# Attention products with W_sa by pairs of row tiles, on rows divided by their denominators when they leave PSUM

## The chip, the cores and the metric

The kernel runs on one core of one Trainium2 chip. The metric is device time in microseconds (us), the median of repeated runs. A profiled execution of the same kernel gives the trace from which all rows below are taken; its clock starts with the first instruction.

The engines are named as the profile names them: PE is TensorE (PEld its weight loads), DVE is VectorE, ACT is ScalarE, POOL is GpSimd, which also issues DMAs, and SP issues DMAs only.

## What is computed

Four graph layers on 2708 nodes with 512 features, one after the other, all in float32. Layers 0 to 2 are of the form "normalize, multiply by the adjacency matrix, multiply by a weight matrix, add". The change lies in layer 3:

```python
h = maximum(layernorm(x), 0)
attn_a = sigmoid(concat([adj @ h, h]) @ Wa.T + ba)          # one gate for each row
attn_b = sigmoid(concat([adj @ h, h]) @ Wb.T + bb)
hW = h @ W_sa
s_left, s_right = hW @ a_sa[0, :512], hW @ a_sa[0, 512:]
e = where(adj != 0, exp(-leaky_relu(s_left[:, None] + s_right[None, :], 0.01)), 0)
attn = e / (sum(e, axis=1) + 1e-5)
x_a = attn @ hW
x_b = adj @ (h @ W_gcnb) + b_gcnb
x = x + sigmoid(attn_a * x_a + attn_b * x_b)
```

The kernel uses that `attn @ (h @ W_sa)` is `(e @ h) @ W_sa` with each row divided by its sum of `e`.

## The kernel before

**Tiles.** The 2708 rows are four quarters (`NQ`) of 677. A quarter holds five full tiles of 128 rows (`KT`), and 37 rows that are left; the rows left of all quarters are gathered in two more tiles, `NF` (4 x 32 rows) and `NF + 1` (4 x 5 rows in 32). A quarter's columns are worked on in two halves (`U`) of 339 (`W`).

**The aggregation.** In each layer `aggregate` forms `adj @ h` by seven outer products instead of eight (a Strassen scheme, `multiply`), into `agg`, which holds the transposed result: features on the partitions, rows of the graph along the free axis. In layer 3 the epilogue of this aggregation is `gated`: for each row tile the products with W_gcnb and the gate vectors. It takes the full tiles two by two: `sums_of_pair` builds four sums of the two tiles' halves, `pair_product` makes seven half products with the weights and with four sums of the weights (`sums_of_w`), and combines them on VectorE (`u2`, `u3`, `c22`, `c21`, `c12`), the first one after a ScalarE copy `v`.

**The attention loop.** `steps` lists 4 quarters x 2 halves x 5 steps. A group is one quarter's half: steps b = 0 to 3 take one block each of 5 x 128 source rows, step b = 4 the tails. `e_step` loads a block of the adjacency (SP's queue, 847.5 KB) and `scores` turns it into `e` in place: ten exponentials on ScalarE (L1215), then two VectorE operations on 128x1695 (L1219, L1220). The loop makes the block of the next step before it multiplies the present one. TensorE multiplies `h` with the block into four PSUM banks `pe` (L1299, 20 matmuls of 339 columns a step), in step 4 the tails (L603, L608). VectorE adds all tiles of `e` into `se` (L1310), which gives the row sums once it is summed over the partitions. At a group's end the four banks go to `agg`, two by VectorE (L1316), two by ScalarE (L1318).

**The row tiles.** A group that ends puts its row tiles on `todo`; each following step takes one. `attention` loads the tile's x and the gated part y, sums `se` by a matmul with one column of ones (L1236), adds eps, takes the reciprocal and multiplies with the gate (L1239 to L1241), multiplies the tile of `agg` with W_sa in four matmuls of 512 columns (L203), and ends with VectorE, tanh on ScalarE, VectorE and the output DMA on POOL's queue (L1246 to L1250):

```python
sm = ps_sm.tile([P, NT], FP, tag="sm", name="pse")
nc.tensor.matmul(sm[:, 0:1], columns(t), ones[:, 0:1], start=True, stop=True)
cs = tile_cols(agg, t)
g = small.tile([P, 1], FP, tag="ge", name="ge")
nc.vector.tensor_add(g, sm[:, 0:1], eps[:, t : t + 1])
nc.vector.reciprocal(g, g)
nc.vector.tensor_mul(g, g, ga[:, t, 0:1])
```

What is left on `todo` after the loop is multiplied then, with `NF + 1` and `NF` put between; the last tile goes in two halves.

**Storage.** PSUM has eight banks: `ps_agg` five, `ps_out` two, `ps_sm` one. The blocks of the adjacency lie in `obuf`, seven places, taken from and given back to the list `free`. In the loop x and y tiles have four places in `ends`.

**Order.** A scheduler places the instructions of each engine; every engine then works through its own list in that order, and waits at an instruction whose inputs or places are not ready.

Of the kernel before, what the change touches and what calls it, by code (L numbers as in the profile page):

```python
# [12 lines left out]
P = 128  # L13
D = 512
# [23 lines left out]
def gnn_kernel(  # L38
# [60 lines left out]
    eps = const.tile([P, NT], FP, name="eps")  # L99
# [13 lines left out]
    ab_rows = dram.tile([NQ, 2, U * W], FP, name="ab_rows")  # L113
# [45 lines left out]
    def full_cols(a, t):  # L159
        k = t % KT  # L160
        return a[:, k * P : (k + 1) * P]
# [52 lines left out]
    def small_cols(tag, n):  # L214

        if n <= KT:
            return small.tile([P, KT], FP, tag=tag, name=tag)
        k = ("rs", "rq", "rv", "rstd", "sh").index(tag)
        return hd[:, :, k] if k < 4 else eps
# [815 lines left out]
    for k in range(2):  # L1035
# [10 lines left out]
    both_places = ends[:, NC * D + 2 * NC :]  # L1046
    w_sums = both_places[:, 0 : 4 * NC // 2 * GW].rearrange("p (k c o) -> p k c o", k=4, c=NC // 2)
    s_places = [
        both_places[:, o : o + 4 * NC // 2 * P].rearrange("p (k c n) -> p k c n", k=4, c=NC // 2)
        for o in (4 * NC // 2 * GW, 4 * NC // 2 * (GW + P))  # L1050
    ]
    w11, w12, w21, w22 = (wg_sb[:, f : f + 2, k] for f in (0, 2) for k in range(2))

    def sums_of_w():
        t1, t2, t3, t4 = (w_sums[:, k] for k in range(4))
        nc.vector.tensor_sub(t1, w12, w11)
        nc.vector.tensor_sub(t2, w22, t1)
        nc.vector.tensor_sub(t3, w22, w12)
        nc.vector.tensor_sub(t4, w21, t2)

    def sums_of_pair(t):
        q = t // KT, (t + 1) // KT
        (a11, a12), (a21, a22) = (
            [agg[:, f, q_ // 2, :, q_ % 2, (t_ % KT) * P : (t_ % KT + 1) * P] for f in range(2)]
            for t_, q_ in ((t, q[0]), (t + 1, q[1]))
        )
        sums_ = take(s_places)
        s1, s2, s3, s4 = (sums_[:, k] for k in range(4))
        nc.vector.tensor_sub(s3, a11, a21)
        nc.vector.tensor_add(s1, a21, a22)  # L1070
        nc.vector.tensor_sub(s2, a22, s3)
        nc.vector.tensor_sub(s4, a12, s2)
        return {1: a11, 2: a12, 3: s4, 4: a22, 5: s1, 6: s2, 7: s3}

    def pair_product(xs_):

        ws = dict(zip((1, 2, 3, 5, 6, 7, 4), (w11, w21, w22, *(w_sums[:, k] for k in range(4)))))

        def part(ps, k, start):
            for c in range(2):  # L1080
                nc.tensor.matmul(
                    ps, xs_[k][:, c], ws[k][:, c], start=start and c == 0, stop=c == 1,
                    skip_group_check=not start,
                )

        def place(tag, bufs=1):
            return upool.tile([P, W], FP, tag=tag, name=tag, bufs=bufs)[:, 0:GW]

        pa, pb, pc, pd = (
            (ps_out if k == 1 else ps_agg).tile(  # L1090
                [P, GW], FP, tag="out" if k == 1 else "agg", name=f"pp{k}"
            )
            for k in range(4)
        )
        part(pa, 1, True)
        v = place("v")
        nc.scalar.copy(v, pa)
        part(pb, 6, True)
        u2 = place("u2", 2)
        nc.vector.tensor_add(u2, v, pb)  # L1100
        part(pa, 2, False)
        part(pc, 7, True)
        u3 = place("u3")
        nc.vector.tensor_add(u3, u2, pc)
        part(pd, 5, True)
        c22 = place("s")
        nc.vector.tensor_add(c22, u3, pd)
        part(pc, 4, False)
        c21 = u3
        nc.vector.tensor_add(c21, u2, pc)  # L1110
        part(pd, 3, False)
        c12 = u2
        nc.vector.tensor_add(c12, u2, pd)
        return [[pa, c12], [c21, c22]]
# [17 lines left out]
    def gated(ts):  # L1132
        ts = list(ts)
        pairs = [t for t in ts if t < NF][::2]
        xs_ = sums_of_pair(pairs[0]) if pairs else None
        for n, t in enumerate(pairs):
            po = pair_product(xs_)
            if n + 1 < len(pairs):
                xs_ = sums_of_pair(pairs[n + 1])
            for k in range(2):  # L1140
                gates(t + k, po[k])
# [19 lines left out]
    def row_scales():  # L1161
# [8 lines left out]
        nc.vector.tensor_scalar(eps, hd[:, :, 0], srmin, None, ALU.add)  # L1170
        nc.vector.scalar_tensor_tensor(eps, eps, 0.01, eps, ALU.mult, ALU.max)
        nc.vector.tensor_sub(dinv, eps, hd[:, :, 0])
        nc.vector.scalar_tensor_tensor(dis, hd[:, :, 0], -0.01, eps, ALU.mult, ALU.add)
        nc.scalar.activation(eps, eps, AF.Exp)
        nc.vector.tensor_scalar(eps, eps, 1e-5, None, ALU.mult)
# [3 lines left out]
            po[: 2 * NT, 0:P], dd[:, 1:3].rearrange("p k t -> p (k t)"), ident,  # L1179
            start=True, stop=True,  # L1180
        )
        r = small.tile([P, P], FP, tag="diag", name="rows", bufs=2)
        nc.scalar.copy(r[: 2 * NT], po[: 2 * NT, 0:P])
        for k in range(2):
# [14 lines left out]
    def column_rows(q):  # L1199
# [4 lines left out]
        for k, r in enumerate((ra, rb)):  # L1204
            nc.vector.memset(r[:, Q : U * W], 0.0)
            nc.gpsimd.dma_start(r[:, 0:Q], ab_rows[q, k, 0:Q].partition_broadcast(P))
# [24 lines left out]
    def attention(t, columns, pieces=1):  # L1231
# [3 lines left out]
        sm = ps_sm.tile([P, NT], FP, tag="sm", name="pse")  # L1235
        nc.tensor.matmul(sm[:, 0:1], columns(t), ones[:, 0:1], start=True, stop=True)  # L1236
        cs = tile_cols(agg, t)
        g = small.tile([P, 1], FP, tag="ge", name="ge")
        nc.vector.tensor_add(g, sm[:, 0:1], eps[:, t : t + 1])  # L1239
        nc.vector.reciprocal(g, g)  # L1240
        nc.vector.tensor_mul(g, g, ga[:, t, 0:1])  # L1241
        n = D // pieces
        for k in range(pieces):
            f = slice(k * n, (k + 1) * n)
            pE = tile_product(t, cs, [wsa_sb[:, c, f] for c in range(NC)])
            nc.vector.scalar_tensor_tensor(y[:, f], pE, g, y[:, f], ALU.mult, ALU.add)  # L1246
            nc.scalar.activation(y[:, f], y[:, f], AF.Tanh, scale=0.5)
            nc.vector.scalar_tensor_tensor(xt[:, f], y[:, f], 0.5, xt[:, f], ALU.mult, ALU.add)
            for o, m, to in place(t):
                nc.gpsimd.dma_start(out[to : to + m, f], xt[o : o + m, f])  # L1250

    sums = misc[:, 0 : 2 * U * W + NQ * (R0 + R1)]
    tail_sums = sums[:, 2 * U * W :].rearrange("p (f i c q r) -> p f i c q r", f=1, i=2, c=1, q=2)
# [14 lines left out]

    steps = [(q, u, b) for q in range(NQ) for u in range(U) for b in range(NQ + 1)]
    lines, ready = {}, None  # L1270

    def gated_and_ready(ts):

        nonlocal ready
        if ts[0] < half:
            sums_of_w()
            return gated(ts)
# [3 lines left out]
        ready = e_step(*steps[0])  # L1281
# [5 lines left out]
    todo = []  # L1287
    for n, (q, u, b) in enumerate(steps):
        cu = slice(u * W, (u + 1) * W)
        se = sums[:, (q % 2) * U * W : (q % 2 + 1) * U * W]  # L1290
        if b == 0:
            pe = [ps_agg.tile([P, W], FP, tag="agg", name=f"pe{c}") for c in range(NC)]
            if u == 1 and q + 1 < NQ:
                lines[q + 1] = column_rows(q + 1)
        (now, blks), ready = ready, e_step(*steps[n + 1]) if n + 1 < len(steps) else None
        if b < NQ:
            for c in range(NC):
                for t, a in now:
                    nc.tensor.matmul(  # L1299
                        pe[c], h[:, t, c * P : (c + 1) * P], a, start=(t == 0), stop=False  # L1300
                    )
        else:
            tail_products(pe, now, False)
            now = [(NF, now[:, 0, :]), (NF + 1, now[:G, 1, :])]
        for t, a in now:
            if t == 0:
                nc.vector.tensor_copy(se[:, cu], a)
            else:
                r = G if t == NF + 1 else P
                nc.vector.tensor_add(se[:r, cu], se[:r, cu], a)  # L1310
        free.extend(blks)
        if b == NQ:
            for c in range(NC):
                d = agg[:, c // 2, q // 2, c % 2, q % 2, cu]
                if c % 2 == 0:
                    nc.vector.tensor_copy(d, pe[c])  # L1316
                else:
                    nc.scalar.copy(d, pe[c])  # L1318
            if u == 0:
                todo += [(t, se) for t in range(q * KT, q * KT + W // P)]  # L1320
            else:
                nc.vector.tensor_copy(tail_sums[:, 0, q // 2, 0, q % 2], se[:, KT * P : Q])
                todo += [(t, se) for t in range(q * KT + W // P, (q + 1) * KT)]
        elif todo:
            t, se_t = todo.pop(0)
            attention(t, lambda t, se_t=se_t: full_cols(se_t, t))
# [3 lines left out]
    todo = [(t, lambda t, se_t=se_t: full_cols(se_t, t)) for t, se_t in todo]  # L1330
    for k, t in ((1, NF + 1), (3, NF)):
        todo.insert(k, (t, lambda t: tile_cols(tail_sums, t, True)[0]))
    for n, (t, columns) in enumerate(todo):
        attention(t, columns, 1 if n + 1 < len(todo) else 2)
# [61 lines left out]
```

## Time and profile before

| | |
|---|---|
| median of three runs | 2083.27 us (2081.92 to 2083.51) |
| the profiled execution's own time | 2079.3 us |
| its span, first to last instruction | 2077.5 us |
| mean granted TensorE clock | 0.998 |
| attention loop, after the gates | about 1614 to 2053 us |
| last matmul of the loop to the end of the span | 24.3 us |

How to read the rows: in a group of instructions stand the line of the kernel, the engine, the operation, the names out<-in, shapes and count, then busy time in us and mean ns of one, then the engine's idle time just before them and what ended it. In a timeline stand start and length in us, and idle time with its releaser in brackets. A float32 matmul leaves two records on PE, so a count of 8 is four matmuls. The ends of matmuls are modelled, so the distance of starts is the better measure of their cost.

### The profile page before, as it was taken

The numbers are of one execution on the slowest core, as the hardware profiler recorded it, in microseconds if no ns is written. First come the engines' busy times: TensorE is split into PE (matmuls) and PEld (weight loads), VectorE is DVE, ScalarE is ACT, GpSimd is POOL, SyncE is SP. The second block draws the span as 40 slices with busy tenths as digits, with TensorE's granted clock in tenths as the row PEclk, the third lists the DMA queues.
The fourth block names the chain that finished last, engine by engine and source line by source line (L and its number), as shares of the span: only waits on it lengthen the run. The fifth ranks groups of instructions, "written<-read, shape, count | busy, mean of one in ns | idle before, by whom it ended". The sixth has DMA issues, their size and how long they took to land.

```text
span 2077.5 us, 19986 instructions
## 1 busy us (share of the span) xinstructions
PE 2035.2 (98%) x7246; PEld 1264.6 (61%) x7246; DVE 1429.1 (69%) x2521; ACT 407.8 (20%) x828; POOL 193.9 (9%) x350
## 2 busy tenths in 40 slices
PE   5999999999999999999999999999999999999998
PEld 2566655656666554666664556666677666666665
DVE  4678877666767778766686889968759755565512
ACT  1430001130000011100002120000117533444411
POOL 0111111120000011100002130001001001000011
PEclk9999999999999999999999999999999999999999
DMA  9998594554445353655444565544552323233220
GB/s 369 304 379 265 184 344 178 190 191 168 168 161 182 137 178 135 238 169 169 160 163 156 197 225 188 175 154 161 188 188 105 119 98 120 93 105 102 96 69 27
DMA packets 80771, 363.65 MB, mean 175 GB/s; under 512 B 11140, under 2 KB 16172, under 8 KB 80544
## 3 DMA queue, kind: packets, MB, share of 16 engines
q1 hardware_dynamic: 50672, 245.43, 33.7%
q0 software_dynamic: 30000, 116.95, 17.3%
q8 instruction: 57, 0.93, 0.2%
q14 instruction: 42, 0.34, 0.1%
HBM read 297.38 MB, written 62.17 MB: 173 GB/s over the span
## 4 chain that ended last, share of the span: by engine, by line
PE 81%; issue 8%; DVE 5%; DMA 5%; POOL 1%; ACT 0%; SPq 0%; POOLq 0%; DVEq 0%; ACTq 0%
PE pe L1299 17%; PE pc L541 13%; PE pa L541 13%; PE pd L541 13%; PE po L203 12%; PE pb L541 6%; DMA obuf<-in_yb_dram 3%; PE pt L603 3%; PE pe L603 1%; PE pt L608 1%; DMA osumt<-ends 1%; DVE ends L1004 1%; DMA ends<-xs 1%; PE dg_ps L324 1%; POOL xbs L1130 0%
## 5 line engine op out<-in xcount | busy, mean ns | idle before, releaser
L1299 PE MATMUL pe<-obuf,h 128*128 128x339 f32 x1280 | 371.4, 448 | 0.0
L1299 PEld LDWEIGHTS pe<-obuf,h 128*128 128x128 f32 x1280 | 241.4, 189 | 130.5 <-issue 12.3
L541 PE MATMUL pa<-obuf,h 128*128 128x339 f32 x1040 | 317.0, 449 | 2.5 <-ACT h L255 1.4
L203 PE MATMUL po<-ends,agg 128*128 128x512 f32 (+1 forms) x648 | 281.1, 590 | 0.3 <-DVE agg L1316 0.3
L541 PEld LDWEIGHTS pa<-obuf,h 128*128 128x128 f32 x1040 | 195.3, 189 | 109.7 <-issue 9.2
L203 PEld LDWEIGHTS po<-ends,agg 128*128 128x128 f32 x648 | 121.3, 190 | 142.7 <-issue 136.5
L1215 ACT ACTIVATE e<-r,nsr 128x339 f32<-128x339 f32 x352 | 171.5, 565 | 54.4 <-DMA r<-ab_rows 15.9
L541 PE MATMUL pb<-t,s 128*128 128x339 f32 x560 | 171.2, 452 | 1.7 <-DVE s L473 0.9
L541 PE MATMUL pc<-t,h 128*128 128x339 f32 x560 | 169.4, 448 | 1.1 <-DVE u L588 1.0
L541 PE MATMUL pd<-t,s 128*128 128x339 f32 x560 | 169.0, 447 | 0.0
L541 PE MATMUL pd<-obuf,s 128*128 128x339 f32 x550 | 166.3, 448 | 0.3 <-DVE agg L562 0.3
L575 ACT COPY v<-pa 128x339 f32<-128x339 f32 x56 | 24.6, 440 | 720.9 <-PE pa L541 694.7
L541 PEld LDWEIGHTS pb<-t,s 128*128 128x128 f32 x560 | 106.2, 191 | 57.3 <-DVE t L513 2.1
L541 PEld LDWEIGHTS pc<-t,h 128*128 128x128 f32 x560 | 105.8, 189 | 56.1 <-DVE u L588 2.2
L541 PEld LDWEIGHTS pd<-t,s 128*128 128x128 f32 x560 | 105.8, 189 | 54.1
L541 PEld LDWEIGHTS pd<-obuf,s 128*128 128x128 f32 x550 | 104.0, 189 | 53.9 <-DVE agg L562 1.1
L541 PE MATMUL pc<-obuf,s 128*128 128x339 f32 x450 | 135.9, 448 | 0.0
L541 PEld LDWEIGHTS pc<-obuf,s 128*128 128x128 f32 x450 | 85.1, 189 | 43.8 <-issue 0.5
L935 POOL DMA_DIRECT2D xs<-ends x66 | 36.0, 546 | 780.8 <-DVE ends L934 705.1
L513 DVE TENSOR_TENSOR t<-obuf,t 128x1695 f32<-128x1695 f32 x55 | 105.3, 1915 | 0.0
L514 DVE TENSOR_TENSOR t<-obuf,t 128x1695 f32<-128x1695 f32 x52 | 99.5, 1914 | 0.1
L1316 DVE COPY agg<-pe 128x339 f32<-128x339 f32 x16 | 7.5, 507 | 133.1 <-PE pe L608 133.1
(290 smaller groups left out, 2280.3 us busy)
## 6 DMA issues: line engine op xcount, KB each, us to landing
obuf<-in_yb_dram SPq DMA_DIRECT2D x132, 847.5 KB, 4.5
obuf<-osumt SPq DMA_DIRECT2D x100, 847.5 KB, 4.4
osumt<-obuf POOLq DMA_DIRECT2D x22, 847.5 KB, 11.3
xs<-ends POOLq DMA_DIRECT2D x66, 256.0 KB, 2.3
ends<-xs POOLq DMA_DIRECT2D x61, 256.0 KB, 3.6
obuf<-in_yt_dram SPq DMA_DIRECT2D x28, 339.0 KB, 3.5
obuf<-in_yb_dram POOLq DMA_DIRECT2D x11, 847.5 KB, 10.9
ends<-in_yb_dram SPq DMA_DIRECT2D x9, 847.5 KB, 9.1
```

The source lines that it names most:

```text
L203: nc.tensor.matmul(po, cs[c], ws[c], start=(c == 0), stop=(c == NC - 1))
L324: nc.tensor.matmul(ps[g], first, y, start=n < 4, stop=n >= len(ops) - 4)
L513: nc.vector.tensor_add(t2, o22, t1)
L514: at_y.append(nc.vector.tensor_add(t4, o21, t2).ins)
L541: last = nc.tensor.matmul(ps, x[:, k, :], y[:, k, :], start=start and k == 0, stop=k == KT - 1, skip_group_check=not start,)
L575: at_v.append(nc.scalar.copy(v, pa).ins)
L603: nc.tensor.matmul(ps[c], h[:, NF, c * P : (c + 1) * P], tl[:, 0, :], start=start, stop=False)
L608: nc.tensor.matmul(ps[c], h[g, NF + 1, c * P : (c + 1) * P], tl[g, 1, :], start=False, stop=True)
L935: nc.gpsimd.dma_start(xs[t], xt)
L1004: nc.vector.tensor_tensor_reduce(y, h[:, t, :], vs[:, k, :], 1.0, 0.0, ALU.mult, ALU.add, hd[:, t, k : k + 1])
L1215: nc.scalar.activation(e[:, k], row, AF.Exp, bias=nsr[:, t, s : s + 1], scale=1.0)
L1299: nc.tensor.matmul(pe[c], h[:, t, c * P : (c + 1) * P], a, start=(t == 0), stop=False)
```

## The change

The full tiles' products with W_sa go by pairs with seven half products, as the gates do. For this the rows have to be divided before the product: a group's sum over the partitions is one matmul of a 128x128 matrix of ones with `se`, its reciprocal `rrow` lies on all partitions, and all four evictions from PSUM become multiplications with it on VectorE. The eps of each row goes with the `ab_rows` into DRAM and is added as a row (`erow`) to `se`. A pair's parts stand between the four main products of one step (`next(pair)`); they use `ps_sm` (`pb`, `pd`, and the sum) and `ps_out` (`pa`, `pc`). The sums of `e` are made as soon as the block is ready, and the tails together with the next group's first block. Two of the seven places of `obuf` hold the sums of W_sa from step 2 on. Six full tiles, `NF + 1` and `NF` are multiplied after the loop, instead of three and these two. The numbers of lines move: the exponentials to L1225, `scores` to L1229 and L1230, the pair's parts to L1077, the results to L1250 to L1256, the main products to L1359, the sum, its reciprocal and the evictions to L1375, L1376 and L1379.

The core of the diff:

```diff
+    def in_four(a):
+        return a.rearrange("p (k c o) -> p k c o", k=4, c=NC // 2)
+    def weights_of_pairs(w, sums):
+        w11, w12, w21, w22 = (w[:, f : f + 2, k] for f in (0, 2) for k in range(2))
+        t1, t2, t3, t4 = sums
         nc.vector.tensor_sub(t1, w12, w11)
         nc.vector.tensor_sub(t2, w22, t1)
         nc.vector.tensor_sub(t3, w22, w12)
         nc.vector.tensor_sub(t4, w21, t2)
+        return {1: w11, 2: w21, 3: w22, 4: t4, 5: t1, 6: t2, 7: t3}
...
-    def pair_product(xs_):
+    def pair_product(xs_, ws, bank):
...
+        pa = bank("pa", n)
         part(pa, 1, True)
         v = place("v")
         nc.scalar.copy(v, pa)
+        pb = bank("pb", n)
         part(pb, 6, True)
         u2 = place("u2", 2)
         nc.vector.tensor_add(u2, v, pb)
+        yield
         part(pa, 2, False)
+        pc = bank("pc", n)
         part(pc, 7, True)
         u3 = place("u3")
         nc.vector.tensor_add(u3, u2, pc)
+        yield
+        pd = bank("pd", n)
         part(pd, 5, True)
         c22 = place("s")
         nc.vector.tensor_add(c22, u3, pd)
+        yield
         part(pc, 4, False)
         c21 = u3
         nc.vector.tensor_add(c21, u2, pc)
         part(pd, 3, False)
         c12 = u2
         nc.vector.tensor_add(c12, u2, pd)
-        return [[pa, c12], [c21, c22]]
+        yield [[pa, c12], [c21, c22]]
...
         nc.tensor.matmul(
-            po[: 2 * NT, 0:P], dd[:, 1:3].rearrange("p k t -> p (k t)"), ident,
-            start=True, stop=True,
+            po[: 3 * NT, 0:P], dd.rearrange("p k t -> p (k t)"), ident, start=True, stop=True
         )
...
-        for k in range(2):
+        for k in range(3):
             for q in range(NQ):
                 t = k * NT + q * KT
                 nc.gpsimd.dma_start(
...
+    def loads(t):
         xt = load_x(t, xs)
         y = load_x(t, xbs)
         nc.scalar.activation(xt, xt, AF.Copy, bias=0.5)
-        sm = ps_sm.tile([P, NT], FP, tag="sm", name="pse")
-        nc.tensor.matmul(sm[:, 0:1], columns(t), ones[:, 0:1], start=True, stop=True)
+        return xt, y
+    def result(t, xt, y, parts, f):
+        for g, c in parts:
+            nc.vector.scalar_tensor_tensor(
+                y[:, g], c, ga[:, t, 0:1], y[:, g], ALU.mult, ALU.add
+            )
+        nc.scalar.activation(y[:, f], y[:, f], AF.Tanh, scale=0.5)
+        nc.vector.scalar_tensor_tensor(xt[:, f], y[:, f], 0.5, xt[:, f], ALU.mult, ALU.add)
+        for o, m, to in place(t):
+            nc.gpsimd.dma_start(out[to : to + m, f], xt[o : o + m, f])
...
+    def pair_bank(name, n):
+        pool, tag = (ps_sm, "sm") if name in ("pb", "pd") else (ps_out, "out")
+        return pool.tile([P, n], FP, tag=tag, name=name)
+    def attention_of_pair(ts):
+        xys = [loads(t) for t in ts]
+        xs_ = sums_of_pair(ts, e_places)
+        yield
+        halves = [slice(k * (D // 2), (k + 1) * (D // 2)) for k in range(2)]
+        for po in pair_product(xs_, ws_e, pair_bank):
+            if po is not None:
+                for t, (xt, y), ps in zip(ts, xys, po):
+                    result(t, xt, y, list(zip(halves, ps)), slice(0, D))
+            yield
...
+        last = n >= len(steps) - NQ - 1
+        pair = None
         if b == 0:
             pe = [ps_agg.tile([P, W], FP, tag="agg", name=f"pe{c}") for c in range(NC)]
+            m = min(W, Q - u * W)
+            nc.gpsimd.dma_start(
+                erow[:, 0:m], ab_rows[q, 0, u * W : u * W + m].rearrange("(o w) -> o w", o=1)
+            )
...
+        elif len(todo) >= 2 and (b == 3 if last else b in (1, 2)):
+            pair = attention_of_pair([todo.pop(0), todo.pop(0)])
+            next(pair)
+            if last:
+                pair, last_pair = None, pair
+        now, blks = ready.pop(0)
         if b < NQ:
+            make_ready(n + 1)
+            if b == NQ - 1:
+                make_ready(n + 2)
             for c in range(NC):
                 for t, a in now:
                     nc.tensor.matmul(
                         pe[c], h[:, t, c * P : (c + 1) * P], a, start=(t == 0), stop=False
                     )
+                if pair is not None:
+                    next(pair)
...
+            else:
+                tl = ready[0][0]
+                sums_of_e(se, [(NF, tl[:, 0, :]), (NF + 1, tl[:G, 1, :])])
+                nc.vector.tensor_add(se[0:1], se[0:1], erow)
         else:
+            ps = ps_sm.tile([P, W], FP, tag="sm", name="pse")
+            nc.tensor.matmul(ps, ones, se, start=True, stop=True)
+            nc.vector.reciprocal(rrow, ps)
             tail_products(pe, now, False)
+            for c in range(NC):
+                nc.vector.tensor_mul(
+                    agg[:, c // 2, q // 2, c % 2, q % 2, cu], pe[c], rrow
+                )
...
-                if c % 2 == 0:
-                    nc.vector.tensor_copy(d, pe[c])
-                else:
-                    nc.scalar.copy(d, pe[c])
...
+        if n == 2:
+            flat = [free.pop(0).rearrange("p k w -> p (k w)") for _ in range(2)]
+            places = [flat[0][:, k * D : (k + 1) * D] for k in range(3)] + [flat[1][:, 0:D]]
+            ws_e = weights_of_pairs(
+                wsa_sb.rearrange("p c (k o) -> p c k o", k=2),
+                [a.rearrange("p (c o) -> p c o", c=NC // 2) for a in places],
+            )
...
-    for n, (t, columns) in enumerate(todo):
-        attention(t, columns, 1 if n + 1 < len(todo) else 2)
+    for _ in last_pair:
+        pass
+    for k in range(2):
+        for _ in attention_of_pair([todo.pop(0), todo.pop(0)]):
+            pass
+        if k == 0:
+            attention(NF + 1)
+    attention(NF, 2)
```

## The prediction

> **What bounds the kernel now.** I read the busy table first, then the slices, then the attention stage by window, by group and in order of time, and the last 25 us in order of time.
>
> ```profile
> PE 2035.2 (98%) x7246; PEld 1264.6 (61%) x7246; DVE 1429.1 (69%) x2521; ACT 407.8 (20%) x828; POOL 193.9 (9%) x350
> ...
> 1617.00:2053.00 436.00, 436.00 (x1517) 273.83 (x1515) 220.08 (x351) 165.23 (x338) 32.91 (x61) 1.00 0.28 92
> ```
>
> The second line is the attention loop: window, TensorE, weight loads, VectorE, ScalarE, POOL, granted clock, DMA share. TensorE is busy in all 436 us at full clock; VectorE in half of them. So in the loop a matmul saved is time saved, as long as nothing new makes TensorE wait. Its course (start, length; two records for each fp32 matmul):
>
> ```profile
> 1993.68 2.44 PE L603 MATMUL pe<-tl,h 128*128 128x339 f32 x8
> 1996.05 0.85 PE L608 MATMUL pe<-tl,h 32*128 32x339 f32 x8
> 1996.83 11.70 PE L1299 MATMUL pe<-obuf,h 128*128 128x339 f32 x40
> 2008.37 0.28 PE L1236 MATMUL pse<-ones,ends 128*128 128x1 f32 x2
> 2008.51 3.68 PE L203 MATMUL po<-ends,agg 128*128 128x512 f32 x8
> 2012.03 11.59 PE L1299 MATMUL pe<-obuf,h 128*128 128x339 f32 x40
> ...
> L1246 DVE SCALAR_TENSOR_TENSOR ends<-po,ge,ends 128x512 f32<-128x512 f32 x17 | 12.7, 746 | 15.0 <-PE po L203 15.0
> ```
>
> A tile's attention takes TensorE from 2008.37 to 2012.03: 0.14 for the sum, 3.52 for four products of 512 columns, 3.66 in all. The last line counts such tiles inside the loop: 17; the other five come after it. A step's 20 matmuls of 339 columns take 11.43 (0.571 each), the two rows of the tails 3.15. The price of a half product stands in the gates, which already work by pairs:
>
> ```profile
> 1500.68 1.03 PE L1081 MATMUL pp<-ends,agg 128*128 128x257 f32 x4
> 1501.55 1.03 PE L1081 MATMUL pp<-ends 128*128 128x257 f32 x4
> 1502.42 1.03 PE L1081 MATMUL pp<-ends,agg 128*128 128x257 f32 x4
> ```
>
> Starts lie 0.87 apart: two matmuls of 257 columns. Now the end:
>
> ```profile
> 2052.34 0.85 PE L608 MATMUL pe<-tl,h 32*128 32x339 f32 x8
> 2067.42 3.70 PE L203 MATMUL po<-ends,agg 128*128 128x256 f32 x16
> ...
> 2063.05 2.02 POOL L1250 DMA_DIRECT2D out_dram<-obuf  x4 [2.12 <-DVE ge L1241]
> 2072.86 0.55 POOL L1250 DMA_DIRECT2D out_dram<-obuf  x1 [0.36 <-DVE obuf L1248]
> ```
>
> The loop's last matmul ends at 2053.2 (call it T0), TensorE's last at 2071.1 (T0+17.9), the span at 2077.5 (T0+24.3), 4.6 after the last output's issue.
>
> **The change, part by part.** The sum is made against the profiled execution (span 2077.5, its own time 2079.3); the median of the runs is 2083.3, 4 higher, and I take the difference over to it.
>
> *Products in the loop.* Before: 17 x 3.66 = 62.2. After: seven pairs (the eighth is begun, but multiplied after the loop), each seven half products of 0.87, 6.07; together 42.5. Added: eight times one matmul of `ones` with `se`, 339 columns, 0.57 as the main matmuls: 4.6. So 47.1: **-15.1**.
>
> *After the loop.* Three pairs, `NF+1` and `NF` stand here now, for five tiles before. TensorE's own work: 18.2 + 2.1 (its rows before, 1.0 and 1.05) + 3.5 = 23.8. In the built order I walk VectorE with the durations of the trace (0.42 for 128x256, pitch 0.35; 0.51 for 128x339, pitch 0.43; 0.48 for a result on 256 columns). The first pair's `u2` is queued behind four evictions, four copies of tail columns and the four sums of the next pair: it ends at T0+4.0, while TensorE has used up `pa`, `pb`, `pa`, `pc` at 3.5 and needs the single `sm` bank: 0.6 lost. `c22` behind `u3` and two more sums costs 0.2, `pa` and `pc` of the third pair 0.2: TensorE ends at about T0+24.8. Last is now `NF` in two halves, each with four output DMAs of 0.51 on POOL; the first four start at T0+25.1 behind its VectorE and ScalarE steps, so the eighth starts at 28.7, and with the same 4.6 the end is T0+33.3: **+9.0**.
>
> *Evictions.* Before, two on VectorE (0.51) and two on ScalarE (0.44); after, four on VectorE, times `rrow`. The next group's first bank is the fifth of `ps_agg`, so its second product, 2.86 after T0, is the first to need an evicted bank, done at T0+0.5. Cost 0, cover 2.3.
>
> *The reciprocal.* Before it has one column (159 ns); now `rrow` has 339. The trace has two that are larger:
>
> ```profile
> 125.72 0.23 DVE L225 RECIPROCAL dd<-hd 128x12 f32<-128x12 f32 x1 [0.29 <-ACT hd L224]
> 154.16 0.28 DVE L225 RECIPROCAL dd<-hd 128x22 f32<-128x22 f32 x1
> ```
>
> Ten more columns cost 55 ns, 5.5 ns each: 0.28 + 317 x 5.5 = 2.0. The Trainium skill speaks against it more loudly: VectorE: DVE Perf Modes, section "Walkthrough: the 8-slice pipeline in each mode", has a reciprocal as an iterative divide with a repeat count of 8; at the page's 0.96 GHz that is 8.3 ns a column, 3.0 in all by this estimate. The low bound is a plain pass, 0.5. It starts when the sum ends, 3.15 before T0, beside the tails. By the row it is ready at T0-1.1, by the page at T0-0.1: both cost nothing. From 3.05 on it delays the end, from 5.4 on also each next group. I take 2.0.
>
> *VectorE's load.* For each group it gains two evictions (1.0), the reciprocal (2.0), the row with eps (0.5), and for a pair 4 sums and 5 combinations of 0.42, 4 results of 0.48 and 2 of 0.69, 7.1, for 3.8 of two tiles' results and small operations. About 6.8 a group, 54 in all, and 2.8 once for W_sa's sums: some 277 of 421, 66%. Not the bound, so 0; what matters is order in its queue (first rival).
>
> *Waits inside a pair's step.* Counted from the step's start on TensorE: `pa`, `pb` end at 4.6, `pa`, `pc` at 9.2, `pd` begins at 12.1, `pc` at 15.8, `pd` again at 16.7. VectorE has first `L1229` for a block whose load can start only when TensorE has freed it at 0 (five blocks now, two hold W_sa's sums). In this stage such loads landed (the loads of `obuf`, 1560 to 2050) in
>
> ```profile
> DMA to landing us min/median/max: 4.1/4.4/4.6
> ```
>
> so `L1229` runs 4.6 to 6.5, `u2` ends at 7.0, `u3` at 10.3, `c22` at 13.5. Needed at 12.1, 15.8 and 16.7. `v` stands on ScalarE behind five exps whose buffer is free before the step: ready at 4.2, needed at 7.5. Cost 0; the smallest cover is 3.2. Each us beyond a cover would come in all seven pairs. Where VectorE itself waits for a pair's part, the scores of later blocks stand behind it; with five blocks these are three steps (34 us) ahead of TensorE, so nothing starves, and a pair's step is 17.5 long.
>
> *The rest, at nothing.* Six more `ab_rows` DMAs (0.54 each on POOL, which is 9% busy and ahead of need by a whole outer product); the `erow` DMA, in POOL's order before the outputs of the pair, issued a group ahead (late, it would hold `se`, the sum on TensorE and all of VectorE's queue, us for us, in eight groups); a pair's four loads, which take all four places and so wait for the last pair's output: free about 6 after a pair, needed a step later. ScalarE's 22 additions and tanhs are as many as before. TensorE's order up to the first attention product is the old one.
>
> **Sum.** -15.1 + 9.0 = -6.1: 2083.3 - 6.1 = **2077.2**.
>
> **Rivals.**
> 1. *Slower: the load ahead of `u2`.* VectorE serves in order, and `u2` frees the only `sm` bank. If the load before `L1229` takes longer than 4.5 + 5.1 = 9.6, `pd` waits, in seven pairs. For it: two blocks fewer, and loads of this size took 9.1 (SP into `ends`) and 10.9 (POOL) earlier in the kernel. Against: 4.4 in this stage at 28% DMA share. At 10.5 the gain is gone (0.9 x 7); at 12 it is 2.4 x 7 = 17 - 6: 2094. Chance 0.10.
> 2. *No change: the combinations hold TensorE a little everywhere.* Before, nothing on TensorE waited for the tile's result; now three links of each pair do, and after the loop nothing covers them. One more us for each pair behind the loop and 0.2 in the loop: 3 + 1.4, 2081.6. For it, one such wait for `v` in the gates:
>
> ```profile
> 1562.81 1.13 PE L1081 MATMUL pp<-ends,agg 128*128 128x257 f32 x4 [1.69 <-ACT v L1097]
> ```
>
> Against: the four pairs that follow it run on without a gap. Chance 0.22.
> 3. *More: the tail costs only TensorE's work.* Without its 1.0 of waits, and with outputs issued 1.5 sooner: 2074.7. Chance 0.08.
>
> The forecast itself (2074.5 to 2079.1) has 0.60.
>
> **Numbers.** 0.2% (4.2 us) is about what a measurement of this kernel can tell from no change. Faster by more: 0.60 + 0.08 = 0.68; within: 0.22; slower: 0.10. The range 2073.8 to 2082.8 takes in the third rival's better half and most of the second.
>
> **What would show it.** In the loop TensorE still at 100%, pairs as rows of four records 0.87 apart between main products, `pse` with 0.57; loop shorter by 15. `L1376` near 2.0, over before the tails' last row. After T0 about 33 instead of 24, one gap of about 0.6 before `pd`. Wrong would be: gaps before `pd` or `pc` in the loop with VectorE's `u2`, `u3` or ScalarE's `v` as releaser (rivals 1, 2), or a reciprocal over 3.

## The result, and the profile after

The changed kernel takes 2076.81 us (median of 16 runs, 2074.32 to 2082.03) against 2082.84 us of the kernel before (16 runs): a ratio of 0.9972, 95% interval 0.9964 to 0.9980, that is 5.8 us less (4.2 to 7.5). The prediction was 6.1 less. The profiled executions have 2074.84 and 2079.3, spans 2073.0 and 2077.5. The spans differ by 4.5 only, since this execution reached the attention loop 0.9 later; 54 us after its start it was already 1.9 behind the other, in instructions that the change doesn't touch. So I compare stages: the loop, from its first main product after the gates to the end of its last tail product (T0), and what lies behind T0.

| | before | after | difference | predicted |
|---|---|---|---|---|
| loop, us | 439.1 | 423.9 | -15.2 | -15.1 |
| T0 to TensorE's last product | 17.9 | 25.0 | +7.0 | +6.9 |
| T0 to the end of the span | 24.3 | 34.1 | +9.8 | +9.0 |
| the two stages | 463.4 | 458.0 | -5.4 | -6.1 |

First the busy table and two windows of the profile after (window, TensorE, weight loads, VectorE, ScalarE, POOL, granted clock, DMA share, GB/s). The second is the loop, the third what follows it:

```profile
PE 2027.9 (98%) x7338; PEld 1285.3 (62%) x7338; DVE 1495.6 (72%) x2593; ACT 406.1 (20%) x822; POOL 202.2 (10%) x367
...
1615.00:2039.00 424.00, 424.00 (x1570) 286.47 (x1569) 277.26 (x406) 164.20 (x333) 36.03 (x67) 1.00 0.30 99
2039.00:2064.00 25.00, 24.64 (x110) 18.68 (x110) 22.15 (x57) 6.11 (x12) 5.31 (x10) 1.00 0.14 53
```

TensorE is busy in all 424 us of the loop at full clock, as it was in the longer one; VectorE went from 223 of 439 to 277 of 424. One pair in the loop, TensorE in order of time (start, length, then line, operation and shapes):

```profile
1948.07 1.02 PE L1077 MATMUL pa<-ends,agg 128*128 128x256 f32 x4
1948.93 1.03 PE L1077 MATMUL pb<-obuf,ends 128*128 128x256 f32 x4
1949.80 3.02 PE L1359 MATMUL pe<-obuf,h 128*128 128x339 f32 x10
1952.66 1.02 PE L1077 MATMUL pa<-ends,agg 128*128 128x256 f32 x4
1953.52 1.03 PE L1077 MATMUL pc<-obuf,ends 128*128 128x256 f32 x4
1954.39 3.02 PE L1359 MATMUL pe<-obuf,h 128*128 128x339 f32 x10
1957.24 1.03 PE L1077 MATMUL pd<-obuf,ends 128*128 128x256 f32 x4
1958.11 3.02 PE L1359 MATMUL pe<-obuf,h 128*128 128x339 f32 x10
1960.97 1.03 PE L1077 MATMUL pc<-obuf,agg 128*128 128x256 f32 x4
1961.83 1.03 PE L1077 MATMUL pd<-ends 128*128 128x256 f32 x4
...
1985.54 0.73 PE L1375 MATMUL pse<-ends,ones 128*128 128x339 f32 x2
```

Seven rows of four records, each 0.87 up to the next row, between main products that leave no gap; `pse` takes 0.57 up to the tails behind it (1986.11). Beside it VectorE, in the same step:

```profile
1950.01 1.93 DVE L1229 SCALAR_TENSOR_TENSOR obuf<-obuf,e 128x1695 f32<-128x1695 f32 x1 [0.96 <-ACT e L1225]
1951.85 0.41 DVE L1092 TENSOR_TENSOR u<-v,pb 128x256 f32<-128x256 f32 x1
...
1954.83 0.41 DVE L1098 TENSOR_TENSOR u<-u,pc 128x256 f32<-128x256 f32 x1
...
1958.31 0.42 DVE L1103 TENSOR_TENSOR s<-u,pd 128x256 f32<-128x256 f32 x1 [1.00 <-PE pd L1077]
```

Subtract the ends from the starts on TensorE and the covers can be read off: `u2` (L1092) ends at 1952.26 and `pd` needs it at 1957.24, 5.0 to spare; `u3` (L1098) at 1955.24 for 1960.97, 5.7; `c22` (L1103) at 1958.73 for 1961.83, 3.1. The end of the last group on VectorE, then the end of the kernel on TensorE and on POOL:

```profile
2035.89 2.28 DVE L1376 RECIPROCAL ends<-pse 128x339 f32<-128x339 f32 x1 [39.80 <-PE pse L1375]
2038.93 0.93 DVE L1379 TENSOR_TENSOR agg<-pe,ends 128x339 f32<-128x339 f32 x2 [0.76 <-PE pe L608]
```

```profile
2042.79 1.13 PE L1077 MATMUL pd<-obuf 128*128 128x256 f32 x4 [0.22 <-DVE u L1092]
2060.25 3.62 PE L203 MATMUL po<-ends 128*128 128x256 f32 x16
```

```profile
2064.38 3.95 POOL L1256 DMA_DIRECT2D out_dram<-obuf  x8 [0.74 <-DVE obuf L1254]
```

The reciprocal is over 0.76 before the tails are. `pd` waits 0.22 behind the loop. The eight outputs of `NF` go out one after the other, 0.49 each, the last from 2067.84 on (T0+28.9), and the span ends 5.1 after that.

### The profile page after: what moved, and what is told of

It is laid out like the page before. It is cut to its first block, busy times and chain, and to the rows that moved or that the text cites. A ratio compares the mean times of both kernels' runs of the same rounds, so it can differ in the third digit from the quotient of the medians.

```text
span 2073.0 us, 20307 instructions
## 1 busy us (share of the span) xinstructions
PE 2027.9 (98%) x7338; PEld 1285.3 (62%) x7338; DVE 1495.6 (72%) x2593; ACT 406.1 (20%) x822; POOL 202.2 (10%) x367
## 4 chain that ended last, share of the span: by engine, by line
PE 88%; DVE 5%; DMA 4%; issue 1%; ACT 0%; POOL 0%; SPq 0%; POOLq 0%; DVEq 0%; ACTq 0%
PE pe L1359 17%; PE pa L541 14%; PE pc L541 14%; PE pd L541 14%; PE po L203 9%; PE pb L541 7%; PE pt L603 3%; DMA obuf<-in_yb_dram 2%; PE pd L1077 2%; PE pa L1077 2%; PE pc L1077 1%; DMA ends<-in_yt_dram 1%; PE pt L608 1%; PE pe L603 1%; PE pb L1077 1%
## 5 line engine op out<-in xcount | busy, mean ns | idle before, releaser
L1359 PE MATMUL pe<-obuf,h 128*128 128x339 f32 x1280 | 373.2, 448 | 0.0
L1359 PEld LDWEIGHTS pe<-obuf,h 128*128 128x128 f32 x1280 | 241.4, 189 | 121.8 <-issue 4.1
L541 PEld LDWEIGHTS pa<-obuf,h 128*128 128x128 f32 x1040 | 196.2, 190 | 110.2 <-issue 10.3
L203 PE MATMUL po<-ends,agg 128*128 128x512 f32 x480 | 207.5, 593 | 0.0
L1225 ACT ACTIVATE e<-r,nsr 128x339 f32<-128x339 f32 x352 | 172.4, 566 | 178.2 <-DVE obuf L1229 87.1
L575 ACT COPY v<-pa 128x339 f32<-128x339 f32 x56 | 24.7, 441 | 719.0 <-PE pa L541 693.0
L203 PEld LDWEIGHTS po<-ends,agg 128*128 128x128 f32 x480 | 90.9, 190 | 114.3 <-issue 109.5
L1229 DVE SCALAR_TENSOR_TENSOR obuf<-obuf,e 128x1695 f32<-128x1695 f32 x32 | 61.5, 1923 | 58.8 <-DMA obuf<-in_yb_dram 39.8
```

The source lines that it names most:

```text
L203: nc.tensor.matmul(po, cs[c], ws[c], start=(c == 0), stop=(c == NC - 1))
L541: last = nc.tensor.matmul(ps, x[:, k, :], y[:, k, :], start=start and k == 0, stop=k == KT - 1, skip_group_check=not start,)
L575: at_v.append(nc.scalar.copy(v, pa).ins)
L1225: nc.scalar.activation(e[:, k], row, AF.Exp, bias=nsr[:, t, s : s + 1], scale=1.0)
L1229: nc.vector.scalar_tensor_tensor(b, b, 0.0, e1[:, :n], ALU.not_equal, ALU.min)
L1359: nc.tensor.matmul(pe[c], h[:, t, c * P : (c + 1) * P], a, start=(t == 0), stop=False)
```

## Experiments

The forecast's theory: the loop gives back TensorE's time, because every new wait has other products in front of it, and behind the loop TensorE's work, small waits and the issue of eight outputs take 9 back. The rivals: VectorE (by its load or its order) holds `pd` and `pc`; the reciprocal is too long; or the gain comes from elsewhere. Comparisons over several runs are given as ratios to the kernel before on the same chip, whose median was 2082.8 to 2084.2; single profiled executions are read by their stages.

### The division alone

```
-        elif len(todo) >= 2 and (b == 3 if last else b in (1, 2)):
-            pair = attention_of_pair([todo.pop(0), todo.pop(0)])
+        if b < NQ and todo:
+            attention(todo.pop(0))
...
+    for k, t in ((1, NF + 1), (3, NF)):
+        todo.insert(k, t)
+    for n, t in enumerate(todo):
+        attention(t, 1 if n + 1 < len(todo) else 2)
```

> The division at the eviction alone: matmul of ones with se, reciprocal of 339 columns, four evictions on VectorE; every tile is multiplied by itself with the whole of W_sa, as before, seven blocks stay in use. My theory: the eight matmuls of 339 columns (8 x 0.57 = 4.6) less the 17 sums of one column that fall away in the loop (17 x 0.14 = 2.4), so +2.2 in the loop, and -0.7 behind it (five such sums): +1.5 against the kernel before, about 2084.3, ratio 1.0007. The pairs alone are then worth about -7.5. If instead the gain came from the division (no scale of the scores' sums by tile, results that read PSUM without it), this kernel is as fast as the changed one, 2077, ratio 0.997, and the pairs are worth nothing. If the four evictions on VectorE hold the next group, +4 or more, with gaps ahead of the main products of a new group.

Measured: ratio 0.9996 (0.9988 to 1.0004; 13 runs, 2083.9), the loop 439.9, from T0 to the end 24.4. The gain is the pairs'. The loop grew by 0.8 where 2.2 was expected. TensorE in order of time, this kernel:

```profile
1954.39 11.60 PE L1354 MATMUL pe<-obuf,h 128*128 128x339 f32 x40
1965.82 3.60 PE L203 MATMUL po<-ends,agg 128*128 128x512 f32 x8
1969.25 11.59 PE L1354 MATMUL pe<-obuf,h 128*128 128x339 f32 x40
```

A tile takes 3.43 here; before, with its sum of one column, 3.66. So that sum cost 0.23 and not the 0.14 between the two starts: the product behind it was 0.09 longer as well. 17 x 0.23 = 3.9 against 8 x 0.57 = 4.6 is the +0.7. It also tells what a pair is worth by itself: 6.07 against 2 x 3.43 = 6.86, so 0.79, and 7.9 of TensorE's work for ten pairs. Most of the loop's -15.2 is work carried out of it: three tiles, 10.3.

### Plain products behind the loop, twice

```
-        elif len(todo) >= 2 and (b == 3 if last else b in (1, 2)):
+        elif len(todo) >= 2 and not last and b in (1, 2):
...
-    for _ in last_pair:
...
+    for k, t in ((4, NF + 1), (7, NF)):
+        todo.insert(k, t)
+    for n, t in enumerate(todo):
+        attention(t, 1 if n + 1 < len(todo) else 2)
```

> Pairs inside the loop only; the six tiles that the three pairs behind the loop multiply are multiplied one by one there. The loop is then the changed kernel's (423.9 by its trace). My theory: TensorE has 26.6 of work behind the loop instead of the changed kernel's 25.0, so the end comes 1.6 later than in the changed kernel: 2078.4. That is: the three pairs keep most of their gain (9 half matmuls' worth, 3.7, of which some 2 goes to waits and to the order of the end). The rival (the pair's chain of combinations, which nothing covers behind the loop, eats its gain there): no difference, 2076.8 within 0.5, or faster.

Measured: ratio 0.9999 (0.9991 to 1.0007), 5.6 above the changed kernel's ratio where 1.6 was expected. The loop is 423.9, all is lost behind it (T0 to the end 41.1, so 7.0 more than in the changed kernel in this execution). POOL and ScalarE, then TensorE in order of time, then two windows of this kernel:

```profile
2058.18 0.54 POOL L916 DMA_DIRECT2D obuf<-xs  x1 [2.35 <-DMA out_dram<-obuf]
2061.17 0.63 ACT L1244 ACTIVATE obuf<-obuf 128x512 f32<-128x512 f32 x1 [2.73 <-DMA obuf<-xs]
```

```profile
2059.07 1.06 PE L206 MATMUL po<-ends 128*32 128x512 f32 x8
2062.84 2.08 PE L210 MATMUL po<-ends,all_again 128*128 128x512 f32 x2 [2.70 <-ACT ends L208]
2064.71 9.19 PE L203 MATMUL po<-ends,agg 128*128 128x512 f32 x16
```

```profile
2060.00:2065.00 5.00, 2.30 (x7) 1.13 (x4) 1.37 (x6) 1.62 (x3) 0.56 (x2) 0.72 0.33 128
2065.00:2070.00 5.00, 5.00 (x8) 1.94 (x8) 1.40 (x2) 0.63 (x1) 2.01 (x4) 0.60 0.05 14
```

A load stands on POOL until an output has left its place; ScalarE, in order, stands in that tile's addition (L1244) until the load has landed, ahead of `NF+1`'s copy (L208); TensorE waits 2.70 for the copy and is granted 0.72 and 0.60 of its clock in these two windows, so that the next two tiles take 9.0 instead of 6.9 (2064.71 to the next row's start at 2073.73). The edit had brought a wait of its own. The second version takes that away:

```
+        elif last and b == 3:
+            early = {t: loads(t) for t in todo[:2]}
...
-        xt, y = loads(t)
+        xt, y = early[t] if t in early else loads(t)
```

> The kernel with pairs inside the loop only once more, with the loads of the first two tiles behind the loop issued in the loop's last step, as the changed kernel does for its last pair; in the first version two loads waited for places that outputs still held, ScalarE stood in those loads ahead of NF+1's copy, TensorE waited 2.7 and was then granted 0.60 of its clock for a while. With that gone, my theory: a plain tile takes 3.43 by the trace of the kernel with the division alone, so six of them 20.6, against 18.2 for three pairs plus some 1.2 of waits: TensorE's end at T0+26.2 against T0+25.0, the whole +1.2 against the changed kernel, ratio to the kernel before 0.9978. The rival (the chain of combinations eats the pairs' gain behind the loop): 0.9972 or less. If the first version's loss was not the load's doing, it stays at 0.9999.

Measured: ratio 0.9982 (0.9974 to 0.9989; 21 runs), 0.0010 or 2.1 us above the changed kernel's; by the traces 2.2 (T0 to the end 36.3 against 34.1, loops equal). Expected was 1.2. TensorE's end came at T0+27.4; the other 1.2 is mostly one wait, here in TensorE's waits from the gates to the end:

```profile
PE po L210 <- ACT ends L208: 1.0, 1, 1.0
```

Without it the kernel is at 26.4, near the 26.2 that I had walked. So by the traces three pairs behind the loop are worth 1.4 even with nothing to cover their combinations, out of 2.4 that TensorE's work gives (3 x 0.79): the rival that these eat all of the gain there falls. The two intervals (0.9964 to 0.9980 and 0.9974 to 0.9989) still touch; the size rests on the traces.

### The outputs on two queues, and other banks

```
-        for o, m, to in place(t):
-            nc.gpsimd.dma_start(out[to : to + m, f], xt[o : o + m, f])
+        for k, (o, m, to) in enumerate(place(t)):
+            queue = nc.sync if t == NF and k % 2 else nc.gpsimd
+            queue.dma_start(out[to : to + m, f], xt[o : o + m, f])
```

> The eight output DMAs of NF alternate between POOL and SP; all else is the changed kernel. My theory: the end is set by the issue of these eight on one queue (0.49 each, the eighth at T0+28.95 by the changed kernel's trace, then 5.1 until the end). On two queues the last issue comes at T0+27.1: -1.9, 2074.9. If the end is set by the landing of the last transfer and not by the queue of issues (the DMA engines serve the eight one after the other at the same pace), no change, 2076.8.

Measured: ratio 0.9957 (0.9944 to 0.9970; 6 runs, 2074.0); loop 423.9, TensorE's end at T0+25.0 as in the changed kernel, the end of the span at T0+32.1 instead of 34.1: -2.0 by the trace, and 1.5 thousandths (3.1 us) by the ratios, whose intervals overlap. POOL now issues two of the second half's four in 0.98, the last of them from 2065.22 (T0+27.3):

```profile
2064.73 0.98 POOL L1257 DMA_DIRECT2D out_dram<-obuf  x2 [0.28 <-DVE obuf L1254]
```

So the queue of issues set the end, and not the transfers one after the other; 4.8 still follow the last issue. The second kernel has this and:

```
+        if behind_loop and name in ("pb", "pd"):
+            return ps_agg.tile([P, n], FP, tag="agg", name=name)
```

> As the kernel with the outputs on two queues, and in addition the products pb and pd of the pairs behind the loop take the banks of ps_agg, which are free there, instead of the single bank of ps_sm, so that pd need not wait for u2 nor the next pair's pb for c12. My theory: the waits behind the loop amount to about 1.2 (25.0 until TensorE's end against 23.8 of work), and most of it goes: TensorE ends near T0+24.0, 0.5 to 1.0 less than with two queues alone, about 2074.2. If the waits come from the combinations themselves (pc after u3, pb after v) and not from the single bank, no difference to two queues alone: 2074.9.

Measured: ratio 0.9953 (0.9941 to 0.9965; 5 runs), TensorE's end at T0+24.7, the span's at T0+31.8: 0.3 less than with two queues alone, less than expected. The wait of `pd` for `u2` is gone, but others remain. TensorE in order of time, this kernel:

```profile
2044.75 1.03 PE L1077 MATMUL pd<-obuf 128*128 128x256 f32 x4
2045.86 1.14 PE L1077 MATMUL pc<-obuf,agg 128*128 128x256 f32 x4
2046.99 1.13 PE L1077 MATMUL pd<-ends,obuf 128*128 128x256 f32 x4
```

Starts lie 1.11 and 1.13 apart, not 0.87: the second `pc` and the second `pd` accumulate in banks that `u3` and `c22` have just read (on VectorE these end at 2045.81 and 2046.93, 0.05 and 0.06 earlier). That is the chain itself. The same kernel on more runs:

> The kernel with the outputs on two queues and the banks of ps_agg behind the loop a second time, on more runs, because its first time rests on five. From the traces it ends 31.75 behind the loop's last matmul and the changed kernel 34.09, with loops of equal length: 2.3 faster than the changed kernel, ratio to the kernel before 0.9972 - 0.0011 = 0.9961. If the first ratio (0.9953) was luck, it is between 0.996 and 0.997; if the outputs on two queues bring nothing beyond the trace's run, 0.9972.

Measured: 0.9963 (0.9951 to 0.9975; 8 runs, 2074.1), T0 to the end 31.8 again. So the first ratio was in part luck, and the ratios alone don't tell this kernel from the one with the outputs on two queues (0.9957). By the traces it ends soonest behind the loop of all versions here, 2.3 sooner than the changed kernel; by this ratio it is 7.7 below the kernel before.

### The reciprocal twice

```
             nc.vector.reciprocal(rrow, ps)
+            nc.vector.reciprocal(rrow, ps)
```

> The reciprocal of 339 columns is issued twice in a row. My theory: 2.28 more on VectorE in each of the eight groups; the first one leaves 0.76 to spare ahead of the end of the tails. In the loop the cover is 3 and more, so its length stays 423.9 within 0.3; behind the loop, where the pairs begin at once, the evictions come 2.28 - 0.76 = 1.5 later and with them u2 and all that follows: the end at T0+35.6 instead of T0+34.1. If the reciprocal were already at its limit in each group, as the estimate of 3.0 would nearly have it, the loop would grow by up to 8 x 1.5 = 12.

Measured: loop 423.91, the changed kernel's to the hundredth; T0 to the end 34.9, +0.8 (1.5 was expected). VectorE and TensorE in order of time, this kernel:

```profile
2040.12 2.28 DVE L1377 RECIPROCAL ends<-pse 128x339 f32<-128x339 f32 x1
2042.51 1.76 DVE L1380 TENSOR_TENSOR agg<-pe,ends 128x339 f32<-128x339 f32 x4
```

```profile
2042.46 1.13 PE L1077 MATMUL pb<-obuf 128*128 128x256 f32 x4 [0.57 <-DVE ends L1377]
```

The second one ends 1.6 after T0 (2040.83), and the evictions begin 1.7 after T0, where in the changed kernel they begin with it. The pair that stands there multiplies tiles of an earlier group, so its products don't need the late columns; `pb` does need the bank that `pse` had, and TensorE begins it 1.70 behind `pa` instead of 0.97: that is nearly all of the 0.8. In the loop the delay is covered, as the prediction had it (to 5.4); what I had not seen is that the first price behind the loop is for `pse`'s bank, not for the evictions.

### VectorE's load

```
-        nc.vector.scalar_tensor_tensor(b, b, 0.0, e1[:, :n], ALU.not_equal, ALU.min)
+        for _ in range(2):
+            nc.vector.scalar_tensor_tensor(b, b, 0.0, e1[:, :n], ALU.not_equal, ALU.min)
```

The second kernel has `range(3)`.

> The first operation of the scores on a block (1.92 each, with no change to its result) is done twice: some 61 us more on VectorE, all of it in the loop, where it is then busy about 340 of 424. My theory: no wait of TensorE, the loop 423.9 within 0.5, since u2, u3 and c22 have 5.0, 5.7 and 3.1 to spare by the changed kernel's trace. If VectorE's load were already what bounds the loop (a second rate beside TensorE's), the loop grows, by up to 7 x 1.9 = 13.

> The same operation three times: some 122 us more, VectorE busy about 400 of 424. My theory: u2 comes 3.85 later and has 5.0 to spare, c22 is at its limit, and a block's chain (scores 7.7, exps 4.8) is about as long as the 13.2 that TensorE takes for a block: 0 to +10 in the loop. If VectorE binds in the loop well before it is full: +20 and more.

Measured: loop 424.9 (+1.0) with VectorE busy 337 of 425, and 430.4 (+6.5) with 387 of 430. TensorE's waits of the second kernel, from the gates to the end:

```profile
PE pe L1360 <- DVE agg L1380: 3.2, 3, 1.4
PE pd L1077 <- DVE s L1103: 2.7, 3, 2.0
```

At 79% load VectorE costs next to nothing (0.8 of the 1.0 is `pd`'s second wait, for `c22`, the smallest cover); at 90% it costs 6. Where it shows first is what the covers say: `c22`, with 3.1 to spare, and the evictions, but not `u2`, which had 3.85 of its 5.0 taken. The load is no second rate in the loop at the change's 65%.

### One wait in doses

`u2` computed 5 and 13 times in each pair of the loop, TensorE's products held in the changed kernel's order; then 13 times with the order left to the scheduler.

```
-        nc.vector.tensor_add(u2, v, pb)
+        for _ in range(times):
+            nc.vector.tensor_add(u2, v, pb)
...
+                with tc.issue_after(of_pair[-1]):
                     for t, a in now:
                         nc.tensor.matmul(
```

> In the seven pairs of the loop u2 is computed five times in a row (no change to its result), with the products of TensorE held in the changed kernel's order, so that nothing steps in where pd waits. In VectorE's order the four repeats take other work between them, so that u2 comes about 4.4 later than in the changed kernel, where it had 5.0 to spare. My theory: no wait, the loop 423.9 within 1. If pd were already at its limit (the wait for the single bank as a rate of its own), the loop grows by 7 x 4.4 = 31.

> The same with u2 computed thirteen times: 12 x 0.33 = 4.0 of repeats and up to 4.8 of other work between them, so u2 ends about 3.7 after the time at which pd is due. My theory, which is the first rival's price beyond its cover: pd waits 3.7 in each of seven pairs, the loop +26, named as a wait of pd for u. If the pairs' waits can be made up later in the step (TensorE has other products to go on with), the loop grows by less than 10.

> u2 thirteen times as before, but with the scheduler free to order TensorE's products: in the order that it makes, pd, pc and pd come eight main products later (4.6 us), behind the first products of the next step. My theory: u2 is there 0.9 before pd, no wait, the loop 423.9 within 1.5, though u2 is as late as in the kernel with the order held. If the lateness of u2 itself were what costs, the loop grows as with the order held, by 26.

Measured: 5 times, no wait in the loop, 424.5 (the 0.6 is one main product more between the loop's bounds); `u2` ends 0.2 to 1.9 ahead of `pd`. 13 times with the order held, 462.3: +38 where 26 was expected. 13 times in a free order, 425.7: +1.8, of which 1.5 is one wait of `pd`. The held kernel, TensorE's waits in the loop and one of the seven in order of time:

```profile
PE pd L1079 <- DVE u L1096: 22.7, 7, 3.9
```

```profile
1671.62 3.02 PE L1365 MATMUL pe<-obuf,h 128*128 128x339 f32 x10
1678.36 2.07 PE L1079 MATMUL pd<-obuf,ends 128*128 128x256 f32 x4 [3.72 <-DVE u L1096]
1680.23 3.60 PE L1365 MATMUL pe<-obuf,h 128*128 128x339 f32 x10
```

The waits are 22.7, 3.2 each, for the 3.7 that I had walked; the order was not held in full, since in four of the seven pairs the next pair's `pa` (0.87) stepped in ahead of the waiting `pd`. Most of the other 15.6 stands in the rows: `pd` takes 2.07 instead of 1.03, and the ten records behind it 3.60 instead of 3.02. The same stretch by windows, with the granted clock third from the end of the row:

```profile
1676.00:1678.00 2.00, 0.00 (x0) 0.00 (x0) 1.83 (x6) 0.00 (x0) 0.00 (x0) 0.99 0.00 0
1678.00:1680.00 2.00, 1.64 (x4) 1.37 (x5) 0.73 (x2) 0.00 (x0) 0.00 (x0) 0.50 0.00 0
1680.00:1682.00 2.00, 2.00 (x7) 1.26 (x6) 0.91 (x2) 0.00 (x0) 0.00 (x0) 0.65 0.00 0
1682.00:1684.00 2.00, 2.00 (x9) 1.40 (x8) 0.00 (x0) 0.00 (x0) 0.00 (x0) 1.00 0.00 0
```

After the wait TensorE runs on at half its clock for about 3 us. From `pd`'s start to that of the next `pc` the seven pairs take 5.3 to 6.3 instead of 3.73 (1957.24 to 1960.97 above), 13.0 in all: 1.9 for each wait, on top of it. The rest of 2.6 is 0.16 more from start to start at each wait than the idle time shows (1.1), one main product more between the bounds as in the kernel with five (0.6), and the eighth pair's first `pa`, which came into the loop (0.9). So the first rival is real as a mechanism, and its place (`pd`'s single bank) and its start (the cover) were right; it is dearer than I had priced it. And it doesn't come about by VectorE being slow alone: where the scheduler may move `pd`, it puts eight main products in front, and the same lateness of `u2` costs 1.8.

## Why the prediction was right, by its steps

- *Products in the loop*: -15.1 predicted, -15.2 measured. Each unit was right: 0.87 for a half product, 6.07 for a pair, 0.57 for `pse`. The division alone was put down at +2.2 in its experiment and is +0.8, since a tile's sum of one column costs 0.23; the prediction had used the whole 3.66 and was not touched by that.
- *Waits in a pair's step*: none in the loop. `u2` had 5.0 to spare (predicted 5.1), `c22` 3.1 (3.2). I had `L1229` wait for its load alone. In four of the seven pairs, the one shown above among them, what it waited for last is ScalarE's exponential (L1225), which ends there at 1950.00, at about the time when the load lands (issued at 1945.41, 4.5 in the median). The time was right, the path only in part. The doses show that these covers are what keeps the loop at 423.9.
- *Reciprocal*: 2.28, between the row's extrapolation (2.0) and the estimate by the Trainium skill, VectorE: DVE Perf Modes, section "Walkthrough: the 8-slice pipeline in each mode" (3.0), nearer to the row. 6.7 ns a column, where ten columns more had cost 5.5 each in the row and the repeat count gives 8.3. Cost nothing, 0.76 to spare before the evictions.
- *VectorE*: 277 busy in the loop, as summed, but in part by luck. The sum put 7.1 for a pair into each of eight groups; with the loop's seven pairs and the 17 tiles of before its own terms give about 271: 222.5 as before, 28 for evictions, reciprocals and eps, 49.7 for pairs, 2.8 for W_sa's sums, less 32.3 for the tiles. The longer reciprocal is 2.3 of what is missing (8 x 0.28); the other 4 stay open.
- *Behind the loop*: +9.8 for +9.0, the only term of the sum that is off by more than 0.1. `pd`'s wait was 0.2 and not 0.6, but TensorE ended at T0+25.0 for 24.8, so most of the waiting stands in small delays elsewhere in the chain. The eighth output's issue came at T0+28.9 for 28.7, and the end 5.1 after it where I had taken the 4.6 of the kernel before, whose last output was one DMA of its own and not the eighth of a row. That is the mis-sized term, 0.5; I can't say from these runs which part of the 5.1 is the transfer's.
- *Rivals*: the first did not come about. The loads of blocks that `L1229` waits for took 4.5 in the median and 6.0 at most, far from the 9.6 at which `pd` would wait; here in the changed kernel's loop, from issue to landing:

```profile
DMA to landing us min/median/max: 4.3/4.5/6.0
```

  Its price was tested by delaying `u2` itself, not by slower loads. The second's waits behind the loop come to 0.2 by name and to 1.2 with all gaps and changes between products (25.0 against 23.8 of work), not to 3, and to nothing in the loop. The third is what two queues for the outputs then made of it, with 2 to gain.
- The sum by the traces is -5.4, against -6.1 predicted; the runs say -5.8, 4.2 to 7.5.

## What to carry to other kernels

A pair with seven half products saves 0.79 of its two tiles' 6.86 here, 11.5% and not an eighth, since a product of 256 columns takes a little more than half of one of 512 (0.433 against 0.857); when the loop gets shorter by more than that, look for what has moved behind it. Write down for each new wait of the busy engine what stands in front of it and by how much it is covered: here the covers (5.0, 5.7, 3.1) said in what order things would fail under load, and a cover that the scheduler makes by ordering is kept only as long as its order is. At the end of a kernel count the issues of DMAs on each queue: eight on one queue were worth 2 us, a fifth of the 9.8 that came back behind the loop.

## What I had not expected of the hardware

A wait of TensorE can cost more than its length. The seven waits of 2.69 to 3.90 us in the kernel with `u2` thirteen times, and the one of 2.70 in the first kernel with plain products, were each followed by half the granted clock, for 3.41 us or twice that. In the first of these kernels 22.7 us of waits cost 35.7 in all (22.7 + 13.0), about 1.6 times their length. A wait of 2.00 in the kernel with the scores three times was followed by full clock:

```profile
1972.03 1.13 PE L1077 MATMUL pd<-ends 128*128 128x256 f32 x4 [2.00 <-DVE s L1103]
1973.00 23.01 PE L1360 MATMUL pe<-obuf,h 128*128 128x339 f32 x80
```

The Trainium skill, TensorE: Matmul & The Clock Gate, section "HAM oscillation — how this bites in real kernels", warns of idle gaps over some 3.4 us; five of these eight waits were shorter, so here the measurement decides. But no limit by length between 2.0 and 2.7 follows. A wait of 1.91 (at 1219.93 in the kernel with the division alone) was followed by half the clock, and one wait of 2.14 or 2.15, for `pt` at 273 to 275 us, stands in ten of the fourteen traces: six go on at full clock, four at half.

What differs is where the wait lies. Within a trace the stretches of half clock start whole multiples of 3.41 us apart. Take windows on that grid (granted clock third from the end). First the kernel with `u2` five times, then that with the division alone, both with a wait of 2.15:

```profile
269.71:273.12 3.41, 1.26 (x5) 0.44 (x5) 3.41 (x5) 0.00 (x0) 0.10 (x1) 1.00 1.03 422
273.12:276.53 3.41, 3.41 (x12) 1.49 (x12) 3.41 (x5) 0.00 (x0) 0.00 (x0) 0.50 1.01 422
...
268.38:271.79 3.41, 1.96 (x12) 0.59 (x4) 3.41 (x9) 0.00 (x0) 0.53 (x1) 1.00 1.03 420
271.79:275.20 3.41, 2.37 (x13) 1.25 (x14) 3.41 (x5) 0.00 (x0) 0.00 (x0) 1.00 1.00 418
```

The first wait (270.86 to 273.00) lies within one window, in which TensorE is busy 37%, and the next window has half the clock. The second (270.68 to 272.83) is cut by the border of two windows, busy 57% and 69%, and the clock stays full. Of the windows at full clock in the fourteen traces, from 200 us to TensorE's end, all twelve with TensorE busy less than 40% were followed by half the clock, and none busy more than 56%; between 42 and 56% both occur. So a wait of some 2 us can halve the clock or not, by where it falls. The kernel with the other banks was traced twice: after its wait for `pt` one execution has half the clock, the other all of it.
